# Preparing the last layer's weights: only the combined blocks ahead of time, the plain ones split on arrival, and their loads on ScalarE's queue

## The chip, the cores and the metric

One core of a Trainium2 chip runs the whole kernel. It has TensorE (PE, matrix products), VectorE (DVE), ScalarE (ACT), GpSimd (POOL) and SyncE (SP, which here only issues transfers). Each engine executes its own instructions in order and waits on semaphores for the others. SBUF is the on-chip working memory, PSUM holds TensorE's results, DRAM is the memory outside the core. The metric is the device time of one execution in microseconds (us); lower is better.

## The reference, cut to what matters

Four sequences of 512 tokens with 1024 features pass through two blocks, each of an attention and a feed-forward part, with a layer norm ahead of each part and a residual sum after it:

```python
x = x + _L0_attn_ref(_layernorm(x))
x = x + _L0_ffn_ref(_layernorm(x), ...)      # routed LoRA, top 2 of 8 per token
x = x + _L1_attn_ref(_layernorm(x), ...)     # 32 heads, causal, low-rank q and kv
x = x + _L1_ffn_ref(_layernorm(x), ...)
```

The change concerns the last one, whose weights are W (1024 x 1024) and A (128 rows in all):

```python
q = x[:, 179:511, :].mean(axis=1)
routing = softmax(q @ router_W.T + router_b)          # one mixture per sequence
base = x @ W.T + b
t = einsum('bsd,erd->bser', x, A)
return base + einsum('bser,eor,be->bso', t, B, routing) * 2.0
```

All numbers are float32. The kernel forms a float32 product from three matmuls of a faster reduced type: each operand is split into a high part, which is the value cast to that type, and a low part, the value less its high part (`matmul3`, lines 131 to 135: low x high, high x low, high x high).

## The kernel before, in words

**Stages.** In the profiled execution, layer 0's attention runs to about 110 us, layer 0's feed-forward (lines 414 to 511) to about 365 us, the projections of layer 1's attention to about 470 us, its heads (lines 712 to 1024) to about 1600 us, and layer 1's feed-forward (lines 1027 to 1260) to the end. The stages overlap where memory allows.

**Who sets the order.** The code is written in a tile language: each tile has a pool, a pool may reuse the memory of an earlier one when its last reader or writer is done, and semaphores are placed automatically. Each engine's order is fixed before the run by a planner that takes what is ready by its own estimate, earliest in the program first. So a transfer can be issued far ahead of its place in the program if nothing holds it: b1T, at line 1140, goes out at 1399 us.

**The last product.** The weights W and A together have 1152 columns. The kernel computes the product by a Winograd form of Strassen's scheme for two problems `s` (each half of the columns): the weights of a problem are cut into four blocks b11, b12, b21, b22 (each of 4 chunks x 128 rows x 288 columns; `W1B` is 288), and seven products with b11, b22, b21 (plain blocks) and t1 = b12 - b11, t2 = b22 - t1, t3 = b22 - b12, t4 = b21 - t2 (combined blocks) stand for eight.

**Preparing the weights.** Layer 0's feed-forward is a loop over 16 tiles of 128 tokens (lines 472 to 511). In its iterations 2 to 9 it also prepares one of eight units `u` (a chunk `c` and a problem `s`) of w1: `fetch_w1` (line 359) loads the unit's four blocks into `room`, an SBUF tile named `raw`; `prepare_w1` (line 366), a generator advanced four times per iteration, forms the combined blocks on VectorE (line 373), casts all seven blocks on ScalarE (line 376), subtracts on VectorE for combined and on POOL for plain blocks to get the low part (line 377), and stores high and low part to DRAM (line 378; `w1_d`). Two output rooms in `raw` take turns. Around it, in the same iteration, the loop runs `base` (the products, TensorE), `route` (small VectorE steps), the bias sum on POOL (line 489) and `finish` (line 324), whose VectorE sum at line 333 takes the result out of PSUM, so that TensorE can use the bank again.

**From the attention into the last stage.** The attention's output is projected by `project` (line 825), a generator called `filler`: it loads pieces of x (`xs`, line 850), casts its operand on ScalarE (`cxh`, line 839), takes the low part on POOL (`cxl`, line 840), multiplies into the banks `poa` and `pob`, adds into `xs` on VectorE (line 878), and stores (line 882). Its last call is spread over lines 1022 to 1125 by `advance(filler, n)`, while the last stage starts: `fetch_h` and `fetch_x` load x for the normalisation and for the output, `load_w1` (line 1037) loads one kind of weight block, high and low part in one transfer of 1152 KB, from SP's queue; `turn1` (line 1059) transposes h; `operands` (line 1076) forms the seven left operands, cast on ScalarE (line 1087) with the low part on POOL (line 1088). The weights of problem 0 are loaded at lines 1105 and 1115, those of problem 1 at line 1134, into memory that the attention's `xs` and weights leave.

**The last loop.** Lines 1222 to 1260 run over 8 pairs `q` of token tiles and the seven `STEPS`. For q = 0 a first pass of the seven steps does problem 0 alone, a second problem 1 alone; from q = 1 each step does both. `product` (line 1194) multiplies and adds the result into xo (`raw` for even q; line 1217) or into `inputs` (the LoRA columns; lines 1213 and 1215). `biased` adds the bias on POOL, `mixture` forms a sequence's routing weights, `weighed` multiplies `inputs` by them, and `lora` adds the LoRA part and stores the output.

Of the kernel before, what the change touches and what calls it, by code (L numbers as in the profile page):

```python
# [9 lines left out]
F32 = mybir.dt.float32  # L10
# [7 lines left out]
P = 128  # L18
# [3 lines left out]
ND = D // P  # L22
# [23 lines left out]
def block_kernel(ctx: ExitStack, tc: tile.TileContext, a: dict, out: bass.AP):  # L46
# [40 lines left out]
    def f32(t):  # L87
        return t.bitcast(F32)
# [260 lines left out]
    def split_shared(pool, ch):  # L349
# [3 lines left out]
        G.tensor_tensor(l, r, f32(h), ALU.subtract)  # L353
        wA.append((h, l))

    w1_d = {(kind, s): dram.tile([P, 2, ND // 2, W1B], F32, name=f"w1_{kind}{s}")
            for kind in KINDS for s in range(2)}

    def fetch_w1(room, u):

# [5 lines left out]
    def prepare_w1(room, u):  # L366

        c, s = divmod(u, 2)
        b11, b12, b21, b22, m1, m2 = (room[:, k * W1B : (k + 1) * W1B] for k in range(6))

        def keep(kind, src, less=None):
            if less is not None:
                V.tensor_tensor(src, less[0], less[1], ALU.subtract)
            n = 6 + 2 * (KINDS.index(kind) % 2)
            h, l = (room[:, (n + k) * W1B : (n + k + 1) * W1B].bitcast(FR) for k in range(2))
            A.copy(h, src)
            (G if less is None else V).tensor_tensor(l, src, f32(h), ALU.subtract)
            nc.sync.dma_start(
                out=w1_d[kind, s][:, :, c, :],
                in_=room[:, n * W1B : (n + 2) * W1B].rearrange("p (k n) -> p k n", k=2))  # L380

        keep("b11", b11)
        keep("t1", m1, (b12, b11))
        yield
        keep("t2", m2, (b22, m1))
        keep("b22", b22)
        yield
        keep("t3", m1, (b22, b12))
        keep("b21", b21)
        yield  # L390
        keep("t4", m2, (b21, m2))
        if u + 1 < ND:
            fetch_w1(room, u + 1)
        yield

    attn = ExitStack()
    cc = attn.enter_context(tc.tile_pool(name="c_const", bufs=1))
# [1 line left out]
    def raw():  # L399
        return rawp.tile([P, ND * NA], F32, name="raw")  # L400
# [13 lines left out]
    with tc.tile_pool(name="b_h", bufs=2) as hp, tc.tile_pool(name="b_hTh", bufs=2) as hTh, \  # L414
# [53 lines left out]
        hts = {0: turn0(0), 1: turn0(1)}  # L468
        po = {0: base(hts[0], w0, W0_COLS, pop, slice(0, 3))}
        room1 = raw()  # L470
        fetch_w1(room1, 0)
        for s, t in enumerate(order):
            prep = prepare_w1(room1, s - 2) if 0 <= s - 2 < ND else iter(())
# [238 lines left out]
    with ExitStack() as c2:  # L712
# [323 lines left out]

        def load_w1(kind, s):
            w = w1[kind, s] = w1p[s].tile([P, 2, ND // 2, W1B], FR, name=f"w{kind}{s}")
            nc.sync.dma_start(out=f32(w), in_=w1_d[kind, s])

        def load_x(q, tiles):
            for t in range(2):
# [12 lines left out]
        def norm(q, t):  # L1055
            s = 2 * q + t
            normalise(hs[q][t], hs[q][t], *stats[s][0], stats[s][1])
# [44 lines left out]
                yield split(a22)  # L1102

        fetch_h(0)
        load_w1(KINDS[0], 0)
        mv = small.tile([P, TPB, 2], F32, name="mv")
        for s in range(TPB):
            V.bn_aggr(mv[:, s, :], stats_d[s])
        mv = mv, rsqrt(mv[:, :, 1], TPB, 1e-5, "rstd")
        stats.update({s: (mv, s) for s in range(TPB)})  # L1110
        norm(0, 0)
        norm(0, 1)
        advance(filler, 3)
        for k in range(1, 7):
            load_w1(KINDS[k], 0)
            advance(filler, 2)
            if k in (2, 3):
                turn1(0, k - 2)
            if k == 4:
                fetch_h(1)  # L1120
                fetch_x(0)
            advance(filler, 2)
        ops = operands()
        parts = [next(ops), next(ops)]
        advance(filler, 28)
# [4 lines left out]
    acc = dp.enter_context(tc.tile_pool(name="d_acc", bufs=1, space=PSUM))  # L1130
    lop = dp.enter_context(tc.tile_pool(name="d_lo", bufs=2, space=PSUM))
    bias1 = broadcast_rows(w1r, a["b1"], D, "bias1")
    for kind in KINDS:
        load_w1(kind, 1)
    rwT = w1r.tile([P, E, ND], F32, name="rwT")
    nc.sync.dma_start(out=rwT, in_=a["rwT"])
# [85 lines left out]
    for q in range(NP):  # L1222
        inputs[q] = wk.tile([P, 2, ER], F32, name="inputs")
        odd, more = q % 2, q + 1 < NP
        if q == 0:
            for step in range(7):
                product(0, step, (0,))
                if step == 2:
                    biased(0)
                if step == 5:  # L1230
                    A.copy(bt1[0], late[:, 0:D])
                    V.tensor_tensor(bt1[1], late[:, 0:D], f32(bt1[0]), ALU.subtract)
        for step in range(7):
            if step == 6 and odd:
                lora(q, 1)
            if step == 1 and more and q + 1 >= TPB // 2:
                st = statistics(hs[q + 1], "d")
                stats.update({2 * (q + 1) + t: (st, t) for t in range(2)})
            if step in (1, 2) and more:
                norm(q + 1, step - 1)  # L1240
            product(q, step, (0, 1) if q else (1,))
            if step == 0 and odd:
                weighed(q - 1, 0)
                weighed(q - 1, 1)
            if step in (1, 2) and odd:
                lora(q - 1, step - 1)
            if step in (3, 4) and more:
                turn1(q + 1, step - 3)
            if step == 3 and more:
                fetch_x(q + 1)  # L1250
            if step == 4 and q + 2 < NP:
                fetch_h(q + 2)
            if step == 5 and more:
                biased(q + 1)
            if step in (4, 5) and odd:
                weighed(q, step - 4)
            if step == 5 and odd:
                lora(q, 0)
            if step == 6 and not odd:
                rw[q // 2] = mixture(sums)  # L1260


# [79 lines left out]
```

## Time and profile before

| | us |
|---|---|
| Median of 3 runs (1842.21 to 1849.34) | 1843.1 |
| The profiled execution's own time | 1845.03 |
| Its span, first to last instruction | 1843.2 |
| TensorE busy in the span | 1739.8 |
| VectorE / ScalarE / POOL busy | 1364.5 / 878.9 / 899.4 |
| Moved by DMA | 230.85 MB on one data queue |

| Stretch, us | TensorE busy | Granted clock | DMA share |
|---|---|---|---|
| 120 to 280: layer 0's feed-forward while w1 is prepared | 148.59 of 160 | 0.99 | 0.50 |
| 280 to 360: the same loop, w1 done | 80.00 of 80 | 1.00 | 0.09 |
| 1557 to 1645: end of the attention, start of the last stage | 66.50 of 88 | 0.86 | 0.79 |
| 1645 to the end | 188.79 of 198.2 | 1.00 | 0.30 |

In the lines of a profile, a group reads: line, engine, operation, output <- inputs, shapes, count | busy time, mean ns of one | idle time of the engine before them and what ended it. A wait reads: engine, the tile it writes, its line <- what ended the wait: us in total, times, the longest. In a chain or a timeline the first two numbers are the start and the duration in us. SPq is SyncE's queue of transfer issues. The granted clock is TensorE's, as a share of full speed.

### The profile page before, as it was taken

Reading aid. Unit: us, or ns where it says so; the run is one execution under the profiler, and the core shown is the slowest. Engines: PE = TensorE matmul, PEld = TensorE weight load, DVE = VectorE, ACT = ScalarE, POOL = GpSimd, SP = SyncE. Lnnn points to the kernel's source line nnn. Section 1 sums busy time; section 2 is a strip of 40 time slices with the busy share of each in tenths; the row PEclk is TensorE's granted clock in tenths of the full one; section 3 lists DMA queues with packets and bytes.
Section 4 is the critical chain, followed back from the end, with each engine's and each line's share of the span. In section 5 each row is a group of like instructions: output and inputs, shape, how many; then the busy total and the mean of one; then the engine's idle time right before and its main releaser. Section 6 shows DMA issues by size and latency. Waiting matters only on the chain.

```text
span 1843.2 us, 30884 instructions
## 1 busy us (share of the span) xinstructions
PE 1739.8 (94%) x10280; PEld 1461.9 (79%) x10280; DVE 1364.5 (74%) x3563; ACT 878.9 (48%) x2290; POOL 899.4 (49%) x808
## 2 busy tenths in 40 slices
PE   6978999999889999999999999999999999689999
PEld 6978999999567778757787757877757777589998
DVE  6777875576787777688777687777678776567685
ACT  6332321155765556465555465555465654232222
POOL 0353221010666666566666566566555564355552
PEclk9989999999999999999999999999999999899999
DMA  4235440134533323343323343333343233862431
GB/s 183 73 130 186 162 172 35 37 98 141 186 95 108 127 93 131 126 143 121 127 93 125 117 158 112 117 110 109 119 146 125 75 104 111 330 238 94 136 117 47
DMA packets 134175, 232.83 MB, mean 126 GB/s; under 512 B 22464, under 2 KB 61376, under 8 KB 130176
## 3 DMA queue, kind: packets, MB, share of 16 engines
q1 hardware_dynamic: 134016, 230.85, 37.1%
q8 instruction: 82, 1.34, 0.3%
q14 instruction: 77, 0.63, 0.1%
HBM read 156.60 MB, written 74.19 MB: 125 GB/s over the span
## 4 chain that ended last, share of the span: by engine, by line
PE 71%; DVE 11%; DMA 6%; POOL 4%; ACT 4%; issue 2%; SPq 0%; ACTq 0%; POOLq 0%; DVEq 0%
PE psv L818 7%; PE pst L802 6%; PE pss L133 3%; PE pss L135 3%; PE pss L134 3%; PE pob L133 3%; PE poa L133 3%; PE psq L133 3%; PE pob L134 3%; PE pob L135 3%; PE psq L135 3%; PE poa L134 3%; PE acc L133 3%; PE poa L135 3%; DMA w_t<-raw 3%; PE psq L134 2%
## 5 line engine op out<-in xcount | busy, mean ns | idle before, releaser
L781 ACT ACTIVATE p<-p,mn 128x512 f32<-128x512 f32 (+3 forms) x512 | 284.1, 557 | 239.7 <-DVE mn L778 239.2
L603 POOL TENSOR_TENSOR qf<-qf,ropeT 64x512 f32<-64x512 f32 x128 | 167.6, 1309 | 205.2 <-ACT qf L599 204.0
L778 DVE CUSTOM_DVE_ANT_0 p<-pss,causal 128x512 f32<-128x512 f32 (+3 forms) x512 | 231.6, 486 | 23.0 <-PE pss L135 19.2
L802 PE MATMUL pst<-ident,p 128*128 128x128 f32 x1280 | 186.0, 275 | 4.9 <-DVE pT L804 4.7
L604 POOL TENSOR_TENSOR qf<-qf,t 64x512 f32<-64x512 f32 x128 | 166.3, 1299 | 45.9 <-DVE t L602 38.6
L802 PEld LDWEIGHTS pst<-ident,p 128*128 128x128 f32 x1280 | 153.9, 142 | 33.1 <-DVE pT L804 7.7
L804 ACT COPY pT<-pst 128x512 f32<-128x512 f32 x256 | 143.6, 577 | 64.5 <-PE pst L802 64.4
L818 PE MATMUL psv<-pT,k 128*64 128x384 f32 (+3 forms) x1024 | 165.5, 443 | 0.0
L133 PE MATMUL pss<-kT,ql 128*128 128x512 f32 (+2 forms) x384 | 143.3, 373 | 22.6 <-POOL ql L612 14.2
L612 POOL TENSOR_TENSOR ql<-qf,qh 128x384 fp32r<-128x384 f32 x128 | 132.8, 1037 | 57.6 <-DVE qh L611 53.1
L840 POOL TENSOR_TENSOR cxl<-s,cxh 128x256 fp32r<-128x256 f32 x128 | 95.6, 748 | 125.7 <-ACT cxh L839 121.9
L133 PE MATMUL po<-w_h,hTl 128*128 128x384 f32 (+1 forms) x384 | 134.4, 350 | 11.4 <-DVE x L333 11.4
L818 PEld LDWEIGHTS psv<-pT,k 128*64 128x64 f32 x1024 | 73.7, 138 | 87.3 <-issue 76.4
L134 PE MATMUL po<-w_l,hTh 128*128 128x384 f32 (+1 forms) x384 | 130.9, 341 | 0.0
L135 PE MATMUL po<-w_h,hTh 128*128 128x384 f32 (+1 forms) x384 | 130.7, 340 | 0.0
L135 PE MATMUL pss<-kT,qh 128*128 128x512 f32 (+2 forms) x384 | 130.6, 340 | 0.0
L134 PE MATMUL pss<-kT,qh 128*128 128x512 f32 (+2 forms) x384 | 130.3, 339 | 0.0
L804 DVE COPY pT<-pst 128x256 f32<-128x256 f32 x128 | 53.9, 421 | 79.2 <-PE pst L802 77.6
L133 PEld LDWEIGHTS pss<-kT,ql 128*128 128x128 f32 x384 | 72.3, 188 | 44.9 <-POOL ql L612 17.8
L599 ACT COPY qf<-psq 128x512 f32<-128x512 f32 x126 | 73.7, 585 | 64.5 <-PE psq L135 64.1
L133 PE MATMUL psq<-qT,wql 128*128 128x512 f32 x252 | 101.7, 403 | 1.9 <-DVE t L602 1.9
L601 DVE TENSOR_TENSOR t<-psq,ropeT 32x512 f32<-32x512 f32 x126 | 87.7, 696 | 19.5 <-ACT qf L599 15.3
(519 smaller groups left out, 4966.5 us busy)
## 6 DMA issues: line engine op xcount, KB each, us to landing
xs<-x_d SPq DMA_DIRECT2D x128, 256.0 KB
x_d<-xs SPq DMA_DIRECT2D x128, 256.0 KB
qT<-q_d SPq DMA_DIRECT2D x16, 1024.0 KB
wo<-in_woT_dram SPq DMA_DIRECT2D x32, 512.0 KB
rb<-r_d SPq DMA_DIRECT2D x128, 128.0 KB
w_t<-raw SPq DMA_DIRECT2D x32, 288.0 KB
wt<-w_t SPq DMA_DIRECT2D x8, 1152.0 KB
x<-in_x_dram SPq DMA_DIRECT2D x16, 512.0 KB
```

The costliest lines, as they stand in the source:

```text
L133: T.matmul(ps, lhsT=al, rhs=bh, start=start, stop=False, **kw)
L134: T.matmul(ps, lhsT=ah, rhs=bl, start=False, stop=False, **kw)
L135: T.matmul(ps, lhsT=ah, rhs=bh, start=False, stop=stop, **kw)
L603: G.tensor_tensor(f[mid], f[mid], ropeT[mid, 0, :], ALU.mult)
L604: G.tensor_tensor(f[mid], f[mid], t2[mid], ALU.add)
L612: G.tensor_tensor(l, f[:, P:S], f32(h), ALU.subtract)
L778: V.tensor_tensor_reduce(out=to, in0=ps[:, 0:n], in1=causal[:, S - n : S], scale=1.0, scalar=-NEG, op0=ALU.add, op1=ALU.min, accum_out=mn[ ...
L781: A.activation(to, to, AF.Exp, bias=mn[:, i : i + 1], scale=-1.0, accum_out=rs[:, i : i + 1])
L802: T.transpose(ps[:, w : w + P], p[:, OF[i] + j * P : OF[i] + (j + 1) * P], ident)
L804: copy(pT[:, AT[js[0]] : AT[js[0]] + w], ps[:, 0:w])
L818: T.matmul(ps[n * KVR : (n + 1) * KVR, S - w : S], lhsT=k[:, j, :], rhs=pTs[u + n][:, AT[j] : AT[j] + w], start=(j == 0), stop=(j == TPB - 1))
L840: G.tensor_tensor(l, src, f32(h), ALU.subtract)
```

## The change

Only the four combined blocks are prepared during layer 0's feed-forward, in the order t1, t3, t2, t4, each formed in place of a block that is no longer needed. Their low parts are all taken on POOL, and three output rooms take turns. The plain blocks are copied unsplit, DRAM to DRAM, into `w1_d` by six transfers from SP. In the last stage, all weight loads are issued from ScalarE's queue, plain blocks first; a plain block (576 KB) is loaded into the place of the low part, cast into the place of the high part by ScalarE, and the difference is taken in place, on POOL for problem 0 and on VectorE for problem 1 (`split_w1`). Around it, `norm`, `fetch_x(0)`, `fetch_h(1)` and the filler's steps change places; `biased(0)` and the split of `bt1` move from the first pass of q = 0 to step 4 of the second; `mixture` moves from step 6 to step 5.

```diff
-    w1_d = {(kind, s): dram.tile([P, 2, ND // 2, W1B], F32, name=f"w1_{kind}{s}")
-            for kind in KINDS for s in range(2)}
+    w1_d = {(kind, s): dram.tile([P, 1 + (kind[0] == "t"), ND // 2, W1B], F32,
+                                 name=f"w1_{kind}{s}") for kind in KINDS for s in range(2)}
...
     def prepare_w1(room, u):
 
         c, s = divmod(u, 2)
-        b11, b12, b21, b22, m1, m2 = (room[:, k * W1B : (k + 1) * W1B] for k in range(6))
-
-        def keep(kind, src, less=None):
-            if less is not None:
-                V.tensor_tensor(src, less[0], less[1], ALU.subtract)
-            n = 6 + 2 * (KINDS.index(kind) % 2)
+        b11, b12, b21, b22 = (room[:, k * W1B : (k + 1) * W1B] for k in range(4))
+        for n, (kind, to, a0, a1) in enumerate((("t1", b11, b12, b11), ("t3", b12, b22, b12),
+                                                ("t2", b22, b22, b11), ("t4", b21, b21, b22))):
+            V.tensor_tensor(to, a0, a1, ALU.subtract)
+            n = 4 + 2 * ((4 * u + n) % 3)
             h, l = (room[:, (n + k) * W1B : (n + k + 1) * W1B].bitcast(FR) for k in range(2))
-            A.copy(h, src)
-            (G if less is None else V).tensor_tensor(l, src, f32(h), ALU.subtract)
+            A.copy(h, to)
+            G.tensor_tensor(l, to, f32(h), ALU.subtract)
             nc.sync.dma_start(
                 out=w1_d[kind, s][:, :, c, :],
                 in_=room[:, n * W1B : (n + 2) * W1B].rearrange("p (k n) -> p k n", k=2))
-
-        keep("b11", b11)
-        keep("t1", m1, (b12, b11))
-        yield
-        keep("t2", m2, (b22, m1))
-        keep("b22", b22)
-        yield
-        keep("t3", m1, (b22, b12))
-        keep("b21", b21)
-        yield
-        keep("t4", m2, (b21, m2))
-        if u + 1 < ND:
-            fetch_w1(room, u + 1)
-        yield
+            if kind == "t4" and u + 1 < ND:
+                fetch_w1(room, u + 1)
+            yield
...
         room1 = raw()
+        for kind in ("b11", "b22", "b21"):
+            row, col = int(kind[1]) - 1, int(kind[2]) - 1
+            for s in range(2):
+                nc.sync.dma_start(
+                    out=w1_d[kind, s][:, 0],
+                    in_=a["w1"][row * ND // 2 : (row + 1) * ND // 2, :,
+                                (2 * s + col) * W1B : (2 * s + col + 1) * W1B].rearrange("c p n -> p c n"))
         fetch_w1(room1, 0)
...
         def load_w1(kind, s):
             w = w1[kind, s] = w1p[s].tile([P, 2, ND // 2, W1B], FR, name=f"w{kind}{s}")
-            nc.sync.dma_start(out=f32(w), in_=w1_d[kind, s])
+            if kind[0] == "t":
+                nc.scalar.dma_start(out=f32(w), in_=w1_d[kind, s])
+            else:
+                nc.scalar.dma_start(out=f32(w)[:, 1], in_=w1_d[kind, s][:, 0])
+
+        def split_w1(kind, s, eng):
+            w = w1[kind, s]
+            A.copy(w[:, 0], f32(w)[:, 1])
+            eng.tensor_tensor(w[:, 1], f32(w)[:, 1], f32(w)[:, 0], ALU.subtract)
...
         fetch_h(0)
-        load_w1(KINDS[0], 0)
+        LOADS = ("b11", "b22", "b21", "t1", "t2", "t3", "t4")
+        for kind in LOADS:
+            load_w1(kind, 0)
...
+        advance(filler, 3)
         norm(0, 0)
         norm(0, 1)
-        advance(filler, 3)
-        for k in range(1, 7):
-            load_w1(KINDS[k], 0)
+        fetch_x(0)
+        advance(filler, 4)
+        for k in range(3):
+            split_w1(LOADS[k], 0, G)
             advance(filler, 2)
-            if k in (2, 3):
-                turn1(0, k - 2)
-            if k == 4:
-                fetch_h(1)
-                fetch_x(0)
+            if k < 2:
+                turn1(0, k)
             advance(filler, 2)
+        fetch_h(1)
...
-    for kind in KINDS:
+    for kind in LOADS:
         load_w1(kind, 1)
...
             for step in range(7):
                 product(0, step, (0,))
-                if step == 2:
-                    biased(0)
-                if step == 5:
-                    A.copy(bt1[0], late[:, 0:D])
-                    V.tensor_tensor(bt1[1], late[:, 0:D], f32(bt1[0]), ALU.subtract)
+                if step > 3:
+                    split_w1(LOADS[step - 4], 1, V)
...
+            if step == 4 and q == 0:
+                biased(0)
+                A.copy(bt1[0], late[:, 0:D])
+                V.tensor_tensor(bt1[1], late[:, 0:D], f32(bt1[0]), ALU.subtract)
...
-            if step == 6 and not odd:
+            if step == 5 and not odd:
                 rw[q // 2] = mixture(sums)
```

## The prediction

> **What bounds the kernel now.** I read the totals first, then the busy time by stretch, then who TensorE waited for in the two stretches where it was not full, then the groups, the chain and SyncE's queue there. The page (busy time; tenths by slice):
>
> ```profile
> PE 1739.8 (94%) x10280; PEld 1461.9 (79%) x10280; DVE 1364.5 (74%) x3563; ACT 878.9 (48%) x2290; POOL 899.4 (49%) x808
> ...
> PE   6978999999889999999999999999999999689999
> ```
>
> TensorE sets the end, so a gain must come out of its gaps. Busy time by stretch (us and count of PE, PEld, DVE, ACT, POOL; clock; DMA share; GB/s):
>
> ```profile
> 120.00:280.00 160.00, 148.59 (x866) 145.37 (x865) 124.34 (x368) 44.34 (x102) 45.89 (x35) 0.99 0.50 167
> 280.00:360.00 80.00, 80.00 (x480) 79.58 (x479) 41.93 (x151) 11.06 (x25) 7.20 (x3) 1.00 0.09 34
> 1557.00:1645.00 88.00, 66.50 (x354) 58.60 (x351) 46.81 (x79) 22.46 (x44) 42.46 (x37) 0.86 0.79 299
> 1645.00:1843.20 198.20, 188.79 (x1352) 181.97 (x1352) 143.72 (x330) 53.53 (x103) 94.27 (x59) 1.00 0.30 102
> ```
>
> The change touches the first row (layer 0's feed-forward while w1 is being prepared) and the third (into the last stage). The first loses 11.4 us; the second row, the same loop without the preparation, is full. The third loses 21.5 us idle and, at a clock of 0.86, about 0.14 x 66.5 = 9.3 us more. Who TensorE waited for, in 100 to 300 and in 1560 to 1645:
>
> ```profile
> PE po L133 <- DVE x L333: 11.4, 8, 3.5
> ...
> PE acc L133 <- DVE raw L1217: 8.0, 1, 8.0
> PE acc L133 <- POOL al L1088: 5.6, 2, 3.8
> PE pob L133 <- DVE xs L878: 5.2, 2, 4.0
> PE pt L318 <- DVE hw L315: 2.2, 1, 2.2
> ```
>
> The first wait: VectorE's adds of line 333, which free the PSUM banks, come late. VectorE's groups in 120 to 280, and the chain at 1600:
>
> ```profile
> L377 DVE TENSOR_TENSOR raw<-raw 128x288 fp32r<-128x288 f32 x32 | 21.7, 682 | 21.8 <-ACT raw L376 21.8
> ...
> 1601.02 0.65 DVE xs L878
> 1601.68 7.43 DMA x_d<-xs
> 1609.23 0.29 DVE inputs L1213
> ```
>
> VectorE spends 21.7 us on low parts and stands 21.8 us before them for ScalarE's casts, which, in ScalarE's own waits for 120 to 270, stand 66.3 us for stores (w_t 38.7, w_b 27.6) that still hold the two output rooms. In-order VectorE passes the delay to line 333. At 1601.68 the attention's last store goes out and takes 7.4 us, behind b21, t4 and two stores on one queue; `inputs` lies where xs lay and can't be written sooner.
>
> **What the Trainium skill says.** "DMA: Bandwidth & Descriptors", Issuing engines are not separate DMA queues: DMAs from any engine share 16 engines; another issuer saves only issue time. The trace agrees as far as it can: DMA share is 1.00 at 393 to 426 GB/s in 1605 to 1630, so moving the loads adds no bandwidth. Same page, Queues, rings and completion order: an engine takes turns between queues packet by packet; so a store on SP's queue would no longer stand behind whole loads on ACT's. Before has one data queue and can't show it. "SBUF — State Buffer", Who interferes with whom: GpSimd and two-input VectorE instructions lock each other out. It agrees: a line 377 on VectorE took 2.60 us beside POOL's 2.40 us bias add at 209.5. "TensorE: Matmul & The Clock Gate", What's actually happening: the clock halves after about 3.4 us idle. Partly: after 3.97 us idle, twelve 512-wide matmuls ran at 0.43 us apart instead of 0.23, but 1.84 us idle also cost.
>
> **Part 1, the preparation.** Per unit, 8 VectorE instructions become 4, 7 casts 4, 7 stores 4; low parts on POOL go from 3 to 4. Over eight units VectorE loses the 32 low parts (21.7 us and the 21.8 us it stood in line), ACT 24 casts x 0.43 = 10 us, SP 24 stores x 0.52 = 12 us; POOL gains 8 x 0.81 = 6.5 us on 45.9 of 160. The outputs rotate over three rooms, so one is reused after three outputs instead of two, with four instead of seven in an iteration of 16 us: casts hardly wait on stores, and nothing on VectorE waits for a cast, so line 333 is in time. I leave 0.8 us (the wait at 277.5, after the preparation), half of the 2.1 us at 214.5 (a burst of statistics) and 1 us for lockouts: 11.4 - 2.9 = **8.5 us**. Ends: 4 and 11.4. The stretch after is full, so it reaches the end. The next unit's fetch still waits for t4's low part, now on POOL (0.81 for 0.46 us): hidden, as VectorE stood 0.3 us for it in all.
>
> **Part 2, the plain blocks.** Six DRAM-to-DRAM copies, 0.59 MB each, go on SP ahead of the first fetch. The trace has no such copy. They depend on nothing, and SP's order is by readiness (b1T of line 1140 went out at 1399), so I place them after x's loads: SP issues nothing from 13.7 to 63.1 and DMA is near 0 from 25 to 60. **0 us**. If they stay at 100 us, 3.5 MB moved at the 170 to 420 GB/s seen would hold up the fetch, b0T and bias0 by 9 to 20 us, partly under matmuls: at most 10 us lost (half of the longer).
>
> **Part 3, into the last stage.** Weight bytes fall from 2 x 8.26 to 2 x 6.49 MB; at 424 GB/s that is 4.2 us of DMA per batch.
> - The store at 1601.68: a 288 KB store in part 1 landed in 2.5 us from issue. I take 3.5 to 4 instead of 7.6: -4, and -1 for a shorter slow clock.
> - 3.97 us at 1587.5, then 2.4 us of slow matmuls: VectorE's xs adds stood behind operand sums that waited for POOL. Seven loads leave SP's line, so xs, stuck until 1577 to 1583, come sooner. The order may just bunch elsewhere; half, -3.
> - 3.8 us at 1627.5 and 25 slow matmuls x 0.11: `biased(0)` held POOL 4.7 us ahead of the low parts and now comes later; line 1068's copies, alternating with POOL, stay. Half, -3. It then stands beside `biased(1)`, 9.4 us of POOL among low parts of 1.3 us: +1.
> - `mixture` one step sooner: TensorE waits 2.2, 1.02 and 1.03 us for hw; half, -2.
> - `norm` behind three steps of the filler: the 1.2 and 0.3 us at 1567 to 1571: -1.
> - New: 14 issues on ACT at SP's 0.45 us = 6.3 us; six casts of 1152 at 1.16 us (512 take 0.62, 1024 1.05); three subtractions on POOL at 2.65 us (1024 take 2.37), three on VectorE at 1.36 us. ACT is idle 65 of these 88 us, POOL 45, VectorE 41, which hides most. But cxh (0.41 us) and cxl, every 1.4 us on TensorE's path, queue behind them on ACT and POOL: +3, from 0 to 15. bt1's cast and `fetch_x`, `fetch_h` change place under this cover: 0.
>
> Sum: -14 + 4 = **-10 us**; ends -25 and +15.
>
> Whole: 8.5 + 10 = 18.5 us. The profiled execution took 1845.0 (span 1843.2 and 1.8 around it), so it becomes 1826.5; it was 1.9 above the median of 1843.1, which becomes **1824.6**.
>
> **Rivals.** (a) Both stretches gain, 1824.6. (b) Only the preparation gains: the last transition is then held by ACT and POOL with the same waits under other names; for it, POOL's 42.5 us gets 8 more. 1843.1 - 8.5 = 1834.6. (c) The transition straightens: the attention finishes first and the store hides under b11, t1, t2 (3 x 1.6 us); of its 30.8 us some 22 come back, 1812.6. Against: DMA is full, and t4 for the second half lands barely in time. (d) Slower: ACT is held by its own issues. SyncE's queue in 1602 to 1626 (start, us):
>
> ```profile
> 1602.42 0.57 SPq L156 DMA_DIRECT2D bias<-in_b_dram  x1
> ...
> 1610.36 0.33 SPq L1136 DMA_DIRECT2D rwT<-in_rwT_dram  x1
> ...
> 1617.20 8.70 SPq L1044 DMA_DIRECT2D xo<-x_d  x4
> ```
>
> Seven loads lie between the first two. rwT goes out just as bias, eight places before it, has landed (POOL's add of bias starts at 1610.50), and xo's four take 8.7 us: a transfer goes out only when the one eight before has landed. On SP that holds nobody. If ACT's loads share the count, each can hold ACT, with cxh, ah, POOL and TensorE behind it, for a landing: 8 x 2.8 us (1.18 MB at 424 GB/s) and 6 x 1.4, 30.8 us in all. Three splits ahead hide 3 x 1.6 = 4.8, and `mixture`, `norm` and the earlier xs still give 4: 1843.1 - 8.5 + 22 = 1856.6. It is slower than before from 17 us held, by over 0.5% from 27. Against: ACT already stood idle 3.5 to 6 us at a time there, so much of a wait may fall into that. (e) It doesn't do what it says: the copies sit at 100 us and eat part 1, and part 3 nets nothing: 1843.
>
> **How the numbers follow.** Chances: (a) 0.50, (b) 0.20, (c) 0.17, (d) 0.09, (e) 0.04. 0.5% is 9.2 us, about what a measurement of this kernel can tell: 1833.9 and 1852.3. Faster: (a) nearly whole, (c), half of (b): 0.76. Same: half of (b), (e), tails: 0.16. Slower: 0.08. The range 1807 to 1840 holds (a), (b), most of (c), and leaves out (d), (e) and the far end of (c). Cases (a) and (c) alone: 1809 to 1832.
>
> **What would show it.** Waits of po on line 333 in 120 to 280 under 4 us, TensorE's share there over 96% (92.9 now); no VectorE wait for the casts. DRAM copies before 63 us. A second data queue; the last x_d store landing within 4 us. POOL's wait share for ah smaller. Wrong if ACT's DMA issues take over 1 us each with cxh waits at 1560 to 1600, or if the copies stand ahead of the fetch at 100 us.

## The result: slower by 1.1%

The changed kernel takes 1866.0 us (median of four runs, 1862.94 to 1868.47) against 1844.2 us for the kernel before on the same chip: a ratio of 1.0113, 95% interval 1.0085 to 1.0141. The prediction said 1824.6, faster, with a chance of 0.08 for slower. The profiled execution took 1862.94 us with a span of 1861.0. It was the fastest of its four: the two profiles lie 17.8 us apart, the medians 21.8, so the profiles place some four fifths of the loss.

The totals and the tenths of the page after (busy us, share of the span, instructions; then the busy share in 40 slices, and the granted clock):

```profile
PE 1739.8 (93%) x10280; PEld 1461.4 (79%) x10280; DVE 1368.1 (74%) x3534; ACT 875.0 (47%) x2272; POOL 913.6 (49%) x819
...
PE   6978999999989999989999999999999998589998
...
PEclk9988999999999999999999999999999999799999
```

TensorE's work is the same to a tenth; the gaps grew. The three stretches of the prediction, in the same columns (us and count of PE, PEld, DVE, ACT, POOL; clock; DMA share; GB/s):

```profile
120.00:280.00 160.00, 145.50 (x835) 143.31 (x834) 113.51 (x325) 34.74 (x79) 53.07 (x44) 0.96 0.36 122
280.00:360.00 80.00, 79.96 (x479) 79.26 (x478) 44.45 (x148) 10.59 (x23) 7.93 (x4) 1.00 0.10 37
1557.00:1645.00 88.00, 55.15 (x278) 44.60 (x277) 47.05 (x62) 24.48 (x43) 43.36 (x34) 0.84 0.66 250
```

Both stretches got worse: 148.6 us busy became 145.5 although VectorE has 11 us less to do there and ScalarE 10, and 66.5 became 55.2. To place the loss I take three marks from the rows of TensorE's tiles: the first pq matmul (it ends layer 0's feed-forward), the last pss matmul (it ends the scores), and the end of the span.

| | first pq | pq to last pss | last pss to end | span |
|---|---|---|---|---|
| before | 373.0 | 1175.0 | 295.2 | 1843.2 |
| after | 378.4 (+5.4) | 1172.8 | 309.8 (+14.6) | 1861.0 |

**Layer 0.** TensorE's and VectorE's waits in 100 to 300 (total us, times, longest), then VectorE's group of subtractions in 120 to 280:

```profile
PE po L133 <- DVE x L333: 13.3, 4, 5.2
...
DVE raw L372 <- DMA raw<-in_w_dram: 9.8, 8, 2.5
```

```profile
L372 DVE TENSOR_TENSOR raw<-raw 128x288 f32<-128x288 f32 x32 | 22.6, 706 | 10.8 <-DMA raw<-in_w_dram 9.8
```

VectorE waits for no cast any more, as forecast. In its place it waits 9.8 us for the fetch of the next unit (0.3 before), and a subtraction takes 706 ns on average instead of 464. TensorE's wait for line 333 grew from 11.4 to 13.3. The eight units, whose subtractions began at 122.0 to 253.1 us before, one unit per iteration of some 16 us, now lie between 121.8 and 198.4, 9.6 us each (count, shortest, median and longest in ns, first and last start in us):

```profile
L372 DVE TENSOR_TENSOR raw<-raw x32: 426/459/1823, 121.8 to 197.4; 128x288 f32<-128x288 f32 x32
```

SyncE's queue shows why the fetch is late:

```profile
153.78 4.63 SPq L377 DMA_DIRECT2D w_t<-raw  x3
158.50 0.56 SPq L363 DMA_DIRECT2D raw<-in_w_dram  x1
...
163.76 6.29 SPq L377 DMA_DIRECT2D w_t<-raw  x4
170.15 1.08 SPq L498 DMA_DIRECT2D x_d<-x  x2
171.27 1.09 SPq L363 DMA_DIRECT2D raw<-in_w_dram  x2
```

A fetch (line 363) stands in SyncE's order behind stores (line 377) that wait for POOL's low parts, and the next subtractions stand behind the fetch.

**Into the last stage.** TensorE's waits in 1560 to 1645:

```profile
PE acc L133 <- POOL al L1091: 19.5, 1, 19.5
PE poa L133 <- POOL cxl L835: 4.4, 2, 4.1
```

What ScalarE did at those two places, DMA issues and casts in order of time (the brackets are idle time before it and its cause):

```profile
1569.51 8.18 ACTq L1035 DMA_DIRECT2D wt<-w_t  x4
1577.79 0.40 ACT L834 CAST cxh<-s 128x256 fp32r<-128x256 f32 x1 [7.89 <-DMA wt<-w_t]
...
1602.85 1.38 ACTq L1037 DMA_DIRECT2D wb<-w_b  x3
1609.24 5.12 ACTq L1035 DMA_DIRECT2D wt<-w_t  x4
1614.46 1.14 ACT L1090 CAST ah<-s 128x512 fp32r<-128x512 f32 x2 [17.22 <-issue]
```

And POOL, which writes al after ah:

```profile
1617.47 2.35 POOL L1191 TENSOR_TENSOR xo<-xo,bias 128x1024 f32<-128x1024 f32 x1 [14.37 <-DMA xo<-x_d]
1624.10 2.34 POOL L1191 TENSOR_TENSOR xo<-xo,bias 128x1024 f32<-128x1024 f32 x1 [4.29 <-DMA xo<-x_d]
1626.40 2.50 POOL L1091 TENSOR_TENSOR al<-s,ah 128x512 fp32r<-128x512 f32 x2
```

Two holds lie one behind the other. ScalarE does not cast while its own DMA issues wait: 7.89 us at the first batch of weights and 17.22 at the second. Of these 17.22, 5.6 pass before the first three loads go out at 1602.85, just after the attention's last product; 5.0 more pass before the fourth, and 5.1 in the last four. When ah is there at 1615, POOL still does not write al: in its fixed order the bias sum of the second pair of tiles, `biased(1)`, stands ahead, and waits for xo's transfer. That is issued as the attention's last store lands, and then shares the DMA engines with the four combined blocks, 4.7 MB (416 GB/s from 1611.5 to 1624). Then TensorE, 19.5 us idle, starts at a clock of 0.50 (1628 to 1633). The chain of waits has the last store and xo's transfer there (start, us):

```profile
1603.61 7.88 DMA x_d<-xs
...
1612.88 11.09 DMA xo<-x_d
```

### The profile page after: what moved, and what is told of

It is laid out like the page before. It is cut to its first block, busy times and chain, and to the rows that moved or that the text cites. A ratio compares the mean times of both kernels' runs of the same rounds, so it can differ in the third digit from the quotient of the medians.

```text
span 1861.0 us, 30786 instructions
## 1 busy us (share of the span) xinstructions
PE 1739.8 (93%) x10280; PEld 1461.4 (79%) x10280; DVE 1368.1 (74%) x3534; ACT 875.0 (47%) x2272; POOL 913.6 (49%) x819
## 4 chain that ended last, share of the span: by engine, by line
PE 70%; DVE 9%; POOL 4%; DMA 3%; ACT 3%; issue 2%; SPq 0%; POOLq 0%; ACTq 0%; DVEq 0%
PE psv L813 7%; PE pst L797 6%; PE pss L133 3%; PE pss L135 3%; PE pss L134 3%; PE po L133 3%; PE po L135 3%; PE po L134 3%; PE pob L133 3%; PE poa L133 3%; PE psq L133 3%; PE acc L135 3%; PE psq L135 2%; PE acc L133 2%; PE psq L134 2%; PE acc L134 2%
## 5 line engine op out<-in xcount | busy, mean ns | idle before, releaser
L773 DVE CUSTOM_DVE_ANT_0 p<-pss,causal 128x512 f32<-128x512 f32 (+3 forms) x512 | 231.7, 487 | 23.3 <-PE pss L135 19.5
L133 PE MATMUL pss<-kT,ql 128*128 128x512 f32 (+2 forms) x384 | 143.8, 374 | 22.0 <-POOL ql L607 13.9
L133 PE MATMUL po<-w_h,hTl 128*128 128x384 f32 (+1 forms) x384 | 135.5, 353 | 13.3 <-DVE x L333 13.3
L596 DVE TENSOR_TENSOR t<-psq,ropeT 32x512 f32<-32x512 f32 x126 | 87.7, 696 | 19.9 <-ACT qf L594 15.6
```

Source lines behind the costliest of these rows:

```text
L133: T.matmul(ps, lhsT=al, rhs=bh, start=start, stop=False, **kw)
L773: V.tensor_tensor_reduce(out=to, in0=ps[:, 0:n], in1=causal[:, S - n : S], scale=1.0, scalar=-NEG, op0=ALU.add, op1=ALU.min, accum_out=mn[ ...
```

## Experiments

Twelve kernels. "Rest" is the time from the last pss matmul to the end, as in the table above. "Less before" is the median less that of the kernel before, run on the same chip; by this the changed kernel stands at +21.8.

| kernel | first pq | rest | median us | less before | ratio to before, 95% |
|---|---|---|---|---|---|
| loads_sp | 379.7 | 299.7 | 1854.3 | +8.6 | 1.0049 (1.003, 1.0068) |
| bias1_late | 379.5 | 306.4 | 1861.0 | +15.3 | 1.0074 (1.0054, 1.0094) |
| low_v | 370.1 | 312.5 | 1859.5 | +13.8 | 1.0066 (1.0047, 1.0086) |
| paced | 363.7 | 310.9 | 1853.1 | +7.4 | 1.0036 (1.002, 1.0052) |
| paced_sp | 366.8 | 299.0 | 1839.7 | -5.5 | 0.9966 (0.9955, 0.9978) |
| paced_v_sp | 359.5 | 299.2 | 1834.5 | -10.6 | 0.9932 (0.9915, 0.9948) |
| moves_only | 372.9 | 299.8 | 1851.4 | +6.3 | 1.0027 (1.0015, 1.0039) |
| paced_sp_old_moves | 366.3 | 301.0 | 1839.1 | -6.0 | 0.9967 (0.9959, 0.9975) |
| loads_after_store | 356.7 | 302.4 | 1836.8 | -10.1 | 0.9949 (0.9929, 0.9969) |
| second_on_act | 356.6 | 310.6 | 1843.6 | -3.3 | 0.9989 (0.9977, 1.0) |
| splits_v | 356.8 | 298.7 | 1831.6 | -15.3 | 0.9924 (0.9903, 0.9944) |
| mixture_back | 358.6 | 294.6 | 1829.7 | -15.6 | 0.9918 (0.99, 0.9935) |

Kernels with the same code up to pq show how far one profile can be read: 378.4 to 379.7 with the change's preparation, 363.7 to 366.8 spaced, 356.6 to 359.5 spaced and with VectorE's low parts. Differences of some 3 us in that column mean nothing. From pq to the last pss all lie between 1172.8 and 1178.3, in a stretch that no edit touches. First pq and rest come from one profiled execution each, which lies up to 3.7 us off its kernel's median; where columns and medians disagree, the text says so.

**1. The loads back on SyncE (loads_sp).**

```diff
-                nc.scalar.dma_start(out=f32(w), in_=w1_d[kind, s])
+                nc.sync.dma_start(out=f32(w), in_=w1_d[kind, s])
```

(and the same for the plain blocks.)

> The changed kernel with one thing undone: all 14 weight loads of the last stage are issued from SyncE's queue again; splits, order and preparation stay. With it the planner also puts the second bias sum back behind the low parts on POOL, as it stood before the change. Theory 1 (ACT held by its own DMA issues, and the bias sum ahead of the low parts): ACT's waits of 7.9 us for a landed weight and of 17.2 us for its issues go, the wait of TensorE for POOL's al (19.5 us) falls under 5 us, the last acc matmul of the w_t kind starts 12 to 18 us sooner than 1856.7, and the time falls from 1866.0 to 1848 to 1854. Theory 2 (the splits of the plain blocks on POOL and VectorE, and their lock, cost the time; the queue is innocent): the splits stay, so the gain is under 4 us, 1862 to 1866. Stage B is the same in both: first pq matmul at 378.

The rest falls by 10.1 us, the median by 11.7 (13.2 by "less before"). ScalarE's two waits are gone, and of TensorE's 19.5 us for al this is left, in 1560 to 1645:

```profile
PE acc L133 <- POOL al L1091: 5.9, 3, 3.3
PE acc L133 <- DVE raw L1222: 5.5, 1, 5.5
```

Theory 1 holds, 0.3 us above its range in time; two of its figures were too bold (5.9 us of waits for al are left instead of under 5, and the last w_t matmul starts 8.0 us sooner, at 1848.7, not 12 to 18). The queue was the larger part of the late loss, but 4.5 us over the kernel before stay, with the splits and the moves still in.

**2. POOL's order alone (bias1_late).**

```diff
             if step == 5 and more:
-                biased(q + 1)
+                with ExitStack() if q else tc.issue_after(lows[-1].ins):
+                    biased(q + 1)
```

`lows` collects the subtractions that write al.

> The changed kernel with POOL's order alone changed: the second bias sum (xo of q=1) is held behind the low parts of the first seven steps. ACT still issues the weight loads. Theory 1a (the 19.5 us wait for al is made by POOL, which stands 18.7 us for xo's transfer ahead of the low part): al comes at about 1617 instead of 1626.4, since ACT's cast of ah comes at 1614.46 all the same; gain 8 to 10 us, 1856 to 1858. Theory 1b (ACT's issue, or the landing of the weights, would have held TensorE as long): TensorE waits as long for ah or for a weight, gain under 3 us, 1863 to 1866.

The rest falls by 3.4 us only, the median by 5.0 (6.4 by "less before"). The wait itself did what 1a said; TensorE at the start of the last stage:

```profile
1620.58 0.61 PE L133 MATMUL acc<-wb,al 128*128 128x288 f32 x1 [8.37 <-POOL al L1091]
```

19.5 became 8.4, the 17.3 us hold of ScalarE stayed, and part of the gain went again later: a wait of 4.2 us for mixture's `each` at 1654. So the 19.5 us were both holds in a row. Neither 1a's 8 to 10 nor 1b's under 3 is right for the whole.

**3. and 4. The preparation (low_v, paced).** low_v puts the low parts back on VectorE; paced spaces the units out.

```diff
-            G.tensor_tensor(l, to, f32(h), ALU.subtract)
+            V.tensor_tensor(l, to, f32(h), ALU.subtract)
```

```diff
-            V.tensor_tensor(to, a0, a1, ALU.subtract)
+            with ExitStack() if n else tc.issue_after(added[-1].ins):
+                V.tensor_tensor(to, a0, a1, ALU.subtract)
```

Here `added` collects line 333's adds, so a unit's first subtraction comes after the last add of the iteration before.

> The changed kernel with the 32 low parts of the preparation back on VectorE instead of POOL. Theory L (the lock between POOL and VectorE makes VectorE late in layer 0): the subtractions fall from 706 to about 464 ns, VectorE's 32 low parts cost some 22 us of its time again, but spread; the first pq matmul comes at 370 to 374 instead of 378.4. Theory F (the units run together at one per 9.5 us, and the next unit's fetch stands on VectorE's path): VectorE still waits about 20 us for raw's fetch and has 22 us more to do; the first pq matmul comes at 378 or later, up to 390. The last stage is the same.

> The changed kernel with the preparation spaced out: the first subtraction of each unit is held on VectorE behind the last line-333 add of the iteration before, so one unit falls into one iteration of some 16 us, as before the change. Theory F (units run together, the fetch on VectorE's path): VectorE's wait for raw's fetch falls from 20.3 us to under 3, TensorE's waits for line 333 from 13.3 us to under 6, the first pq matmul comes at 364 to 371 instead of 378.4, and the time falls by 7 to 14 us. Theory L (the lock with POOL): spacing does nothing to the count of POOL's low parts; subtractions stay near 700 ns, waits for line 333 stay over 10 us, first pq at 376 to 380. The order of the later stages is planned anew, so the time can differ by some us more; the first pq matmul is what tells.

In each run the theory that it was built for came true, so the two are not rivals but parts. (The 20 us of waiting for the fetch that both texts start from is not in the trace of the changed kernel; 9.8 is.) VectorE's groups of low_v in 120 to 280:

```profile
L376 DVE TENSOR_TENSOR raw<-raw 128x288 fp32r<-128x288 f32 x32 | 16.9, 530 | 3.3 <-ACT raw L375 2.9
L372 DVE TENSOR_TENSOR raw<-raw 128x288 f32<-128x288 f32 x32 | 15.0, 470 | 8.8 <-DMA raw<-in_w_dram 8.6
```

The subtractions are back at 470 ns, VectorE still waits 8.6 us for the fetch, though the stores ahead of it no longer wait for POOL's low parts, and pq starts 8.3 us sooner. (VectorE took 32 low parts on itself, 16.9 us, and got 7.6 us of the subtractions back: its sum is larger, yet TensorE waits less for line 333, 7.2 us.) In paced the fetch is never waited for; TensorE's wait in 100 to 300, the place of the subtractions, and the stretch of the prediction:

```profile
PE po L133 <- DVE x L333: 4.4, 2, 2.4
...
L374 DVE TENSOR_TENSOR raw<-raw x32: 441/453/936, 158.6 to 271.4; 128x288 f32<-128x288 f32 x32
```

```profile
120.00:280.00 160.00, 155.59 (x927) 154.24 (x926) 117.03 (x357) 36.82 (x83) 57.51 (x44) 1.00 0.35 117
```

TensorE is 97.2% busy, and pq starts 14.7 us sooner than in the changed kernel and 9.3 sooner than before the change. The edit does two things, though: it spaces the units, and it starts them 37 us later. The longest wait for line 333 in the changed kernel lies before that start:

```profile
148.74 0.70 PE L133 MATMUL po<-w_h,hTl 128*128 128x392 f32 x1 [5.23 <-DVE x L333]
```

The kernel before has one of 3.50 us there as well. How much of the gain is the spacing and how much the later start was not tried apart. The subtractions of paced take 534 ns on average, with all low parts still on POOL, so most of what the 706 ns have over the 464 went with the bunching.

**5. Both (paced_sp),** and **6. with VectorE's low parts (paced_v_sp).** No new edits: 1 and 4 together, then 1, 3 and 4.

> The changed kernel with both earlier edits together: preparation spaced out, and the weight loads issued from SyncE. If the two losses add up: first pq matmul at 364 as in the spaced run, 1173 to 1175 us from there to the last pss matmul, 299.7 us from there to the end as with the loads on SyncE, so a span of 1837 to 1839 and a time of 1838 to 1841, 3 to 7 us below the kernel before (1845.65 in the last runs). If the earlier end of layer 0 is given back in the transition (as the spaced run gave back some of it by its medians), 1844 or more.

> As the run with spacing and loads on SyncE, but the 32 low parts of the preparation on VectorE. If the lock between POOL and VectorE still costs when the units are spaced, the first pq matmul comes before 363, by up to 8 us. If the lock cost only because VectorE was the late engine, the 17 us of VectorE's own work cost as much or more: first pq at 363 to 370, and TensorE's waits for line 333 are 4.4 us or more. The rest stays as in that run.

The losses add up: 1839.7, inside the expected 1838 to 1841. With the low parts on VectorE no wait for line 333 is left before pq, pq starts another 7 us sooner, and 1834.5 beats the kernel before by 0.7%. The first alternative holds: POOL's low parts cost even when spaced. Of the 7 us the subtractions themselves make 2.7 (450 ns instead of 534); where the others lie was not traced.

**7. and 8. The moves (moves_only, paced_sp_old_moves).** moves_only is the kernel before with this alone:

```diff
             for step in range(7):
                 product(0, step, (0,))
-                if step == 2:
-                    biased(0)
-                if step == 5:
-                    A.copy(bt1[0], late[:, 0:D])
-                    V.tensor_tensor(bt1[1], late[:, 0:D], f32(bt1[0]), ALU.subtract)
...
+            if step == 4 and q == 0:
+                biased(0)
+                A.copy(bt1[0], late[:, 0:D])
+                V.tensor_tensor(bt1[1], late[:, 0:D], f32(bt1[0]), ALU.subtract)
...
-            if step == 6 and not odd:
+            if step == 5 and not odd:
                 rw[q // 2] = mixture(sums)
```

paced_sp_old_moves is the reverse on kernel 5.

> The kernel before, with the moves of part 3 alone: first bias sum and bt1 into step 4 of the second pass, mixture one step sooner; preparation, loads and queues as before. If the moves are worth what the prediction gave them (bias sum 3 less 1, mixture 2): 4 us less from the last pss matmul to the end, 291 instead of 295.2, and 1841 to 1842. Rival: the bias sums then stand together among the low parts and VectorE's mixture stands ahead of the operand sums, so nothing or a loss up to 5 us: 1846 to 1850.

> As the run with spacing and loads on SyncE, with the bias sum, bt1 and mixture back at their places of before. With the loads on SyncE the transition still took 299.7 us, 4.5 more than before. If the moves make these 4.5 us: 295 to 296 us from the last pss matmul to the end, 4 us below the other run. If the splits of the plain blocks make them (VectorE's three of 3.7 us beside POOL): no change within 1 us, or a loss of up to 4.

The moves lose on the kernel before: rest 299.8 for 295.2, median 1851.4, the rival's loss and 1.4 us above its range. POOL, and TensorE behind it:

```profile
1628.58 2.34 POOL L1186 TENSOR_TENSOR raw<-raw,bias 128x1024 f32<-128x1024 f32 x1 [1.99 <-DVE raw L1217]
1630.87 1.26 POOL L1088 TENSOR_TENSOR al<-a,ah 128x512 fp32r<-128x512 f32 x1
1633.41 1.78 POOL L1088 TENSOR_TENSOR al<-a,ah 128x512 fp32r<-128x512 f32 x1 [1.28 <-DMA xo<-x_d]
```

```profile
1635.24 0.61 PE L133 MATMUL acc<-wb,al 128*128 128x288 f32 x1 [6.76 <-POOL al L1088]
```

The wait of 3.80 us that moving the bias sum was to shorten became 6.76: the moved sum now stands ahead of the last two low parts before that wait ends, where nothing stood before. TensorE's waits for mixture's `each` grew too, from 0.6 to 3.2 us in 1525 to the end, and those for hw did not fall (4.3 and 4.2). Yet putting all three back in kernel 5 gains nothing (rest 301.0 for 299.0, medians within 0.5). Beside the splits of the plain blocks, the old places are no better as a set.

**9. The store (loads_after_store).** On kernel 6: the seven loads of the second half are issued after `inputs` is written. A memset of one column of the first block, which its load then overwrites, makes the wait.

```diff
+            if s and kind == LOADS[0]:
+                with tc.issue_after(copied[-1].ins):
+                    V.memset(f32(w)[:, 1, 0, 0:1], 0.0)
...
                 product(0, step, (0,))
+                if step == 1:
+                    for kind in LOADS:
+                        load_w1(kind, 1)
```

> As the run with spacing, VectorE's low parts and loads on SyncE (1834.5), but the seven loads for the second half wait until the attention's last x_d store has landed and inputs is written. The prediction had that store land in 3.5 to 4 us once it had a queue of its own; on its own queue it took 7.9 us, and ahead of the loads on one queue 4.99 us with the loads going out beside it. If the bytes in flight beside it set its landing, it lands in 2.3 to 3 us now, TensorE's wait for VectorE at the start of the last stage falls from 5.6 to 3 to 3.6 us, and 299.2 us from the last pss matmul to the end become 295 to 297, as long as b11 lands before the second pass. If something else than bytes (the write itself) takes the 5 us, the wait stays over 5 us and the loads come later: 300 us or more.

The first expectation fails: TensorE's wait there is 4.9 us. The chain of kernel 6, and the chain of this one (start, us):

```profile
1594.22 4.99 DMA x_d<-xs
```

```profile
1588.04 4.29 DMA x_d<-xs
...
1593.03 5.10 DMA wb<-w_b
```

With no weight load in flight the store still takes 4.3 us, and part of that is another transfer: in every kernel with the changed preparation SyncE issues the load of bias, 512 KB, right ahead of the store, and the packet records of this run have bias from 1588.3 to 1591.3 and the store's own packets from 1590.4 to 1592.0. The loads behind it on the same queue cost it 0.7 us in kernel 6, and nothing in kernels 11 and 12, where 4.3 us pass from its issue to the next write of `inputs` (4.4 here). Holding them costs more: their first block takes 5.1 us from its issue, now after the store, and the rest grows to 302.4.

**10. Which hold (second_on_act).** Kernel 6 with `(nc.scalar if s else nc.sync).dma_start` in both branches of `load_w1`.

> As the run with spacing, VectorE's low parts and loads on SyncE (1834.5), but the second batch of seven loads is issued from ACT again, the first stays on SyncE. It parts the two holds of ACT: 7.9 us at the first batch, 17.2 us at the second. If the second (with the bias sum that then comes ahead of the low parts on POOL) made most of the loss: 299.2 us from the last pss matmul to the end become 305 to 311, and the time 1841 to 1846. If the first batch made it: 299 to 301, 1835 to 1837.

The rest is 310.6, +11.4 us, but its profile is 3.7 us over the median; by "less before" the second batch costs 7.3 us, of the 13.2 that both cost in loads_sp. So it makes most of the loss. TensorE, and POOL ahead of it, show the picture of the changed kernel again:

```profile
1620.65 0.61 PE L133 MATMUL acc<-wt,al 128*128 128x288 f32 x1 [12.40 <-POOL al L1093]
```

```profile
1610.37 3.10 POOL L1193 TENSOR_TENSOR xo<-xo,bias 128x1024 f32<-128x1024 f32 x1 [18.64 <-DMA xo<-x_d]
1617.04 2.34 POOL L1193 TENSOR_TENSOR xo<-xo,bias 128x1024 f32<-128x1024 f32 x1 [3.56 <-DMA xo<-x_d]
1619.33 2.49 POOL L1093 TENSOR_TENSOR al<-a,ah 128x512 fp32r<-128x512 f32 x2
```

What the first batch, which held ScalarE 7.9 us and TensorE 4.1, adds to it stays open: nothing by the rest (10.1 us for both batches, 11.4 for the second alone), up to 6 us by the medians.

**11. and 12. The remaining 4 us (splits_v, mixture_back).** On kernel 6:

```diff
-            split_w1(LOADS[k], 0, G)
+            split_w1(LOADS[k], 0, V)
```

and on top of it, for the last kernel:

```diff
-            if step == 5 and not odd:
+            if step == 6 and not odd:
                 rw[q // 2] = mixture(sums)
```

> As the run with spacing, VectorE's low parts and loads on SyncE (1834.5), but the first batch's three plain blocks get their low parts on VectorE instead of POOL (2.65 us each there and 5.4 in pairs with the lock). If POOL's splits stand ahead of cxl and al: TensorE's wait of 3.3 us for al at 1574 and of 1.9 us for the sums go, 2 to 5 us less from the last pss matmul to the end, 294 to 297. Rival: VectorE's xs adds come later by the 1.36 us of each split, and the waits for xs (5.4 us) grow by as much: 298 to 301.

> As the run with spacing, loads on SyncE and every low part of preparation and first splits on VectorE (1831.6), with mixture alone one step later again, where it stood before the change. If the earlier mixture stands ahead of the operand sums on VectorE and so delays hw (TensorE waited 5.4 us for hw and 1.6 for each in 1610 to 1630; before the change 2.2 and none): 295 to 297 us from the last pss matmul to the end instead of 298.7, and 1828 to 1830. If mixture's place is worth nothing either way, since its chain of small instructions is as long in both: 298 to 300, 1831 to 1833.

splits_v: TensorE's longest wait for al fell from 3.3 us to 2.1, its waits for hw grew from 3.9 to 5.4, and the rest is the same, 298.7, as the rival had it. The median is 2.9 us lower (4.7 by "less before"); the profile shows no place for that but pq's start, within that column's scatter. mixture_back: the rest falls by 4.1 us to 294.6, and TensorE's waits for hw in 1525 to 1700, 5.4 us in splits_v, read

```profile
PE pt L318 <- DVE hw L315: 1.0, 1, 1.0
```

though one for `each` of 4.2 us is new (1.6 in all before). The medians don't bear the 4.1 out: this one is 1.9 us lower, 0.3 by "less before", and the stretch from pq to the last pss is 3.6 us longer in this profile than in that of splits_v. That mixture's earlier place cost time in this kernel is not shown. The kernel takes 1829.7 us, 0.8% under the kernel before (0.65 to 1.0%): the change, with its preparation spaced, its low parts there and in the first splits on VectorE, its loads on SyncE, and mixture where it was.

## Why the prediction was wrong, step by step

**Part 2, the copies: right.** They went out at the first moment SyncE had free:

```profile
14.51 10.75 SPq L462 DMA_DIRECT2D w_b<-in_w_dram  x6
```

Nothing waits for them; 0 us.

Part 1 is the one that left its stated ends (a gain of 4 to 11.4 us); part 3 stayed just inside its own (-25 to +15).

**Part 1, the preparation: -8.5 forecast, +5.4 measured.** The mechanism (VectorE freed of low parts and of waits for casts, so line 333 in time) is right as far as the casts go, and the size is reached once the units are held to their iterations: paced has -9.3 against before, a wait for line 333 of 4.4, 97.2% busy. Some of that may be luck: the later start was no part of the forecast, and 3.5 of the 11.4 us of wait before the change lay ahead of it. The step that failed is "The next unit's fetch still waits for t4's low part, now on POOL (0.81 for 0.46 us): hidden, as VectorE stood 0.3 us for it in all". The 0.3 us was a reading of a kernel whose units were spaced out. With the change the units ran together, and the fetch came onto VectorE's path (9.8 us, and 8.6 even with the low parts on VectorE). That the output rooms, which held ScalarE 66 us before, were the brake fits both traces, but no run put the two rooms or the seven outputs back. The second failed term is "1 us for lockouts": beside POOL's low parts the 32 subtractions took 706 ns instead of 464, 7.7 us in all, and with the low parts on VectorE pq starts 8.3 us sooner. That GpSimd and two-input VectorE instructions lock each other out is what the Trainium skill says in "SBUF — State Buffer", Who interferes with whom, and these runs agree; what I did not do is count how often the two would meet.

**Part 3, into the last stage: -10 forecast, +14.6 measured.**

- The 14 issues and splits, "+3, from 0 to 15": the issues alone cost 10.1 us by the rest and 13.2 by the medians (loads_sp), inside the term's ends. Rival (d) named the mechanism, ScalarE held by its own issues with cxh, ah, POOL and TensorE behind it, and priced the holds at 30.8 us, 4.8 of them hidden; I gave it 0.09. Of its two holds the second did most of the harm. What no case had is that POOL's order would be planned around it, with `biased(1)` ahead of the low parts and bound to a transfer beside the weights: 3.4 of the 10.1 us (bias1_late). The sentence "ACT is idle 65 of these 88 us ... which hides most" is where it went wrong: idle time of an in-order engine covers work, not a wait at the wrong place. The sign of being wrong that the prediction named came true: four issues spread over 8.18 us at 1569.5, and cxh waiting 7.89 behind them. Whether each hold ends with the landing of the transfer eight places before, as (d) has it, was not tried.
- The store, "3.5 to 4 instead of 7.6": it took 7.88 us on its own queue. The 2.5 us it was drawn from was a store of part 1, in a stretch with a DMA share of 0.50; here the share is 0.93, and bias, 512 KB, goes out on SyncE's queue right ahead of it. The Trainium skill's "DMA: Bandwidth & Descriptors", Queues, rings and completion order, says that a DMA engine turns between queues packet by packet. I read it as help for the store. It cuts the other way too, and the packet records agree: in the changed kernel the plain blocks move on ScalarE's queue from 1604.5 on, bias takes from 1603.9 to 1608.2 beside them, and the store's packets end at 1610.8, 7.2 us after its issue. In kernel 6, with the loads behind both on one queue, bias takes from 1594.8 to 1598.2, and the store's packets end at 1598.8, 4.6 us after its issue. The gain that I put down to the second queue comes with the loads on SyncE.
- The xs wait of 3.97, "half, -3": it is gone in the changed kernel, but the waits for xs make 5.5 us in all as before (2.9 and 2.6 in 1560 to 1645, 5.2 and 0.3 before), and with the loads on SyncE one of 4.2 is back. It bunched elsewhere, as the step feared.
- `biased(0)`, "-3" and "+1": 3.80 became 6.76 us in moves_only.
- mixture, "-2": no gain that a run shows. Put back alone, it changed the rest by -4.1 us and the median by -0.3 to -1.9.
- `norm`, "-1": not tried alone.

The sum of the late part: 10.1 for the queue and POOL's order with it, and 4.5 more. On the kernel before, the moves alone cost as much (4.6); but with the splits in, putting them back did nothing, so how these 4.5 lie between mixture, the bias sum and the splits in the changed kernel stays open.

**The chances.** (d) was what happened late, while the preparation lost instead of gaining; 1856.6 for (d) was short by 9.4 us. It counted -8.5 for the preparation (+5.4 came, 13.9 of difference) and -4 for mixture, norm and xs, which no run shows, and 26 us for the holds where 10 to 13 came. That it lies no farther off is luck: its errors went opposite ways.

## What to carry to other kernels

Before a wait is removed, ask what it may have paced: the stores that held two output rooms were a cost on the page, and with them gone the units ran together. After such a change, bind the work to its place by an explicit order; here that won back more than layer 0 had lost. Do not give DMA issues to an engine whose next instruction feeds the bottleneck: it is not the issue's 0.3 to 0.5 us that counts but where its wait stands in that engine's order. And a moved instruction is judged by the one behind it on its engine: the bias sum, moved "out of the way", came to stand ahead of low parts that TensorE waited for.

## What the runs showed of the hardware

- From the issue of the last 256 KB store to the next write of `inputs`, 7.8 to 8.1 us pass in the five kernels with the second batch of loads on ScalarE's queue (after, bias1_late, low_v, paced, second_on_act), and 4.3 to 5.1 in the seven that have that batch on SyncE's queue, behind the store. In before and moves_only, with loads ahead of it on the one queue, it is 7.4 to 7.6. A queue of its own did not make this store land sooner.
- VectorE's 128x288 subtractions took 706 ns on average with POOL's low parts beside them in bunched units, 534 in spaced ones (paced), and 470 and 450 with those low parts on VectorE (low_v, paced_v_sp). 16.9 us of added VectorE work made TensorE's start of the next stage 8.3 us earlier.
- After 1.84 us of idle time, TensorE's 288-wide matmuls in the kernel before start 0.24 us apart instead of 0.13, from 1582.8 to 1586.1, at a granted clock of 0.50.
- Two losses in stages 1200 us apart added up to within 1 us (expected 1838 to 1841, measured 1839.7).
